# Carrying transposed squares through a DRAM tile with four writes and one read, in place of sixteen SBUF to SBUF transfers

## The chip, the cores and the metric

One core of one Trainium2 chip. The metric is the time of the whole program on the device in microseconds (us), the median of several runs. The program uses one core.

## The reference, cut to what matters

Four graph layers over x of shape (32, 512, 128), all float32. The kernel works on *pairs* of batch items, 16 pairs. Each layer normalizes a pair to h and needs h both with nodes on the partitions (for the products with the adjacency) and with features on the partitions (hT, for the products with weights).

```python
for layer in (L0, L1, L2, L3):
    h = jnp.maximum(_layernorm(x, axis=-1), 0.0)
    x = x + layer(h, adj, ...)
# L0: A*I h W0 + A*(1-I) h W1 ; L1: relu([h, A^T h, (2AA-I)^T h, ...] Theta + b)
# L2: phi2(relu(phi1([ (adj*adj)^T relu(h psi), h ]))) ; L3: tanh/exp attention over h q k^T h^T, masked by adj
```

## The kernel before

`transposed` turns h into hT. VectorE transposes 32x32 squares in place into `hb` (two buffers), and transfers on the SP queue then carry row block i, column block j of the squares to row block j of `hT` (four buffers of 512 KB). That takes sixteen transfers of 32 KB for each of 60 pairs: pairs 4 to 15 of layer 0 (the first four are transposed by TensorE), and all pairs of layers 1 to 3.

```python
def transposed(h, name):
    hb = late.tile([P, NQR, 2, NT, QR], F32, tag="hb", name=f"hb_{name}", bufs=2)
    for b in range(2):
        nc.vector.transpose(hb[:, :, b]..., h[:, b]...)                      # L227
    hT = feature_major(name)                                                 # bufs=4
    for i in range(NQR):
        for j in range(NQR):
            nc.sync.dma_start(hT[j * QR : (j + 1) * QR, i], hb[i * QR : (i + 1) * QR, j])   # L232
    return hT
...
def cross_rows(dst, src):                    # 16 transfers on the same queue, called twice before layer 0
    for a in range(NT):
        for b in range(NQR):
            nc.sync.dma_start(dst[a * QR : (a + 1) * QR, b, :], src[b * QR : (b + 1) * QR, a, :])   # L96
...
def layer0_first(q):
    ln_stats(q);  yield
    h = normed(q);  yield
    hT = (transposed_by_pe if q < EARLY else transposed)(h, f"hT0_{q}");  yield
    g = ...                                  # p_g = hT W1, then evicted to g
    early[q] = hT, g
def layer2(q):
    ...; feat = relu(p_feat + psib)          # p_feat = hT psi: VectorE, then ScalarE
    msgT = mixed(feat, ...)                  # p_msgT on TensorE
    nc.gpsimd.tensor_add(xt[q], xt[q], phi2b[...])
```

In these traces every engine and queue takes its instructions in the order that the compile step gave them; that order follows the program only roughly.

Of the kernel before, what the change touches and what calls it, by code (L numbers as in the profile page):

```python
# [9 lines left out]
F32 = mybir.dt.float32  # L10
# [5 lines left out]
P = 128  # L16
QR = 32
NQR = P // QR
# [6 lines left out]
def kernel(  # L25
# [33 lines left out]
    nc = tc.nc  # L59
# [11 lines left out]
    bounce = ctx.enter_context(tc.tile_pool(name="bounce", bufs=4, space=bass.MemoryType.DRAM))  # L71

    def bank(name):
        return psum.tile([P, 512], F32, tag="bank", name=name)
# [135 lines left out]
    def feature_major(name):  # L210
        return work.tile([P, NQR, 2, P], F32, tag="hT", name=name, bufs=4)
# [10 lines left out]
    def transposed(h, name):  # L222


        hb = late.tile([P, NQR, 2, NT, QR], F32, tag="hb", name=f"hb_{name}", bufs=2)
        for b in range(2):
            nc.vector.transpose(hb[:, :, b].rearrange("p j t r -> p t j r"),  # L227
                                h[:, b].rearrange("p t (j c) -> p t j c", c=QR))
        hT = feature_major(name)
        for i in range(NQR):  # L230
            for j in range(NQR):
                nc.sync.dma_start(hT[j * QR : (j + 1) * QR, i], hb[i * QR : (i + 1) * QR, j])  # L232
        return hT

    def mixed(h, mat, tag, name, copy):
# [26 lines left out]
    def layer0_first(q):  # L262
        ln_stats(q)
        yield
        h = normed(q)
        yield
        hT = (transposed_by_pe if q < EARLY else transposed)(h, f"hT0_{q}")
        yield
        g = work.tile([P, NT, 2, D], F32, tag="g", name=f"g_{q}", bufs=4)
        for b in range(2):  # L270
            pg = projected(f"p_g_{q}_{b}", (at(hT, b), w0[:, 1, :]))
            nc.vector.tensor_copy(g[:, :, b, :], pg)
        early[q] = hT, g
# [144 lines left out]
    p = bank("p_adiag")  # L418
# [15 lines left out]
    p = bank("p_qk_t")  # L434
# [4 lines left out]
    p = bank("p_qk")  # L439
# [36 lines left out]
    def layer1(q):  # L476
        h = normed(q)
        yield
        hT = transposed(h, f"hT1_{q}")
        yield  # L480
        x1T, x2T, hs = [], [], []
        for b in range(2):
            x1T.append(mixed(h[:, b], adj_s, "mT", f"x1T_{q}_{b}", nc.vector.tensor_copy))
            x2T.append(mixed(h[:, b], cheb, "x2T", f"x2T_{q}_{b}", nc.scalar.copy))
            hs.append(straight(hT, b, None, f"hs_{q}_{b}"))
        yield
        for b in range(2):
            po = projected(f"p_l1_{q}_{b}", (columns(hs[b]), th[:, 0, :]), (columns(x1T[b]), th12[:, 0, :]),
                           (columns(x2T[b]), th12[:, 1, :]))
            y = late.tile([P, NT, D], F32, tag="y", name=f"y1_{q}_{b}", bufs=3)  # L490
            nc.vector.tensor_add(y, po, spread(b1, NT))
            nc.vector.scalar_tensor_tensor(xt[q][:, b], y, 0.0, xt[q][:, b], OP.max, OP.add)
        ln_stats(q)

    def layer2(q):
        h = normed(q)
        yield
        hT = transposed(h, f"hT2_{q}")
        yield
        yield  # L500
        feat = []
        for b in range(2):
            pf = projected(f"p_feat_{q}_{b}", (at(hT, b), psi))
            feat.append(late.tile([P, NT, D], F32, tag="y", name=f"feat_{q}_{b}", bufs=3))
            nc.vector.tensor_add(feat[b], pf, spread(psib, NT))
            nc.scalar.activation(feat[b], feat[b], AF.Relu)  # L506
        yield
        msgT = [mixed(feat[b], sq[0], "mT", f"msgT_{q}_{b}", nc.vector.tensor_copy) for b in range(2)]
        nc.gpsimd.tensor_add(xt[q], xt[q], phi2b[:, None, None, :].to_broadcast([P, 2, NT, D]))
        yield  # L510
        h1T = []
        for b in range(2):
            ph = bank(f"p_phi1_{q}_{b}")
            nc.tensor.matmul(ph, phi1[:, 1, :], hT[:, :, b, :], start=True, stop=False)  # L514
            nc.tensor.matmul(ph, phi1[:, 0, :], msgT[b], start=False, stop=True)  # L515
            h1T.append(late.tile([P, N], F32, tag="x2T", name=f"h1T_{q}_{b}"))
            nc.scalar.activation(crossed(h1T[b]), split(ph), AF.Relu, bias=phi1b)
        yield
        for b in range(2):
            po = projected(f"p_l2_{q}_{b}", (columns(h1T[b]), phi2))  # L520
            nc.vector.tensor_add(xt[q][:, b], po, xt[q][:, b])
        ln_stats(q)
# [94 lines left out]
```

## Time and profile before

| | before |
|---|---|
| time, median of 4 runs | 1077.55 us |
| span of the profiled run | 1075.6 us |
| TensorE (PE) busy | 1033.2 us, 96% |
| wait of p_g for hT / of p_msgT for feat | 7.2 us / 7.9 us |
| VectorE's wait for a free hb | 105.0 us |
| SP queue for the squares of a pair | 16 issues, 10.35 us |

TensorE is the bound, so time can change only where TensorE stands still or runs at half rate after standing still. The prediction shows the lines. One more view is used throughout: the length of each stage, read from TensorE's timeline as the distance between the first instruction of one stage and the first of the next (first p_l, first p_x1T, first p_feat, p_feat of the second pair, first p_qkh, end). It includes idle and half-rate time, so a difference of stage lengths is a gain or loss of time, and the differences add up to that of the spans.

### The profile page before, as it was taken

The numbers are of one execution on the slowest core, as the hardware profiler recorded it, in microseconds if no ns is written. First come the engines' busy times: TensorE is split into PE (matmuls) and PEld (weight loads), VectorE is DVE, ScalarE is ACT, GpSimd is POOL, SyncE is SP. The second block draws the span as 40 slices with busy tenths as digits, with TensorE's granted clock in tenths as the row PEclk, the third lists the DMA queues.
The fourth block names the chain that finished last, engine by engine and source line by source line (L and its number), as shares of the span: only waits on it lengthen the run. The fifth ranks groups of instructions, "written<-read, shape, count | busy, mean of one in ns | idle before, by whom it ended". The sixth has DMA issues, their size and how long they took to land.

```text
span 1075.6 us, 14578 instructions
## 1 busy us (share of the span) xinstructions
PE 1033.2 (96%) x4966; PEld 701.7 (65%) x4966; DVE 551.7 (51%) x1280; ACT 413.0 (38%) x877; POOL 233.9 (22%) x214
## 2 busy tenths in 40 slices
PE   4998899999999999999969999999999999999997
PEld 3567799995565655656545555555567777677775
DVE  8924566543243332423433554566676565655443
ACT  5723233501221322213642434322265464655543
POOL 2334244322000000001430111000013232333232
PEclk9898999999999999999989999999999999999999
DMA  9512111110101010010110111111111122122201
GB/s 269 127 47 69 51 51 51 51 52 19 27 25 35 20 34 26 25 34 20 51 29 26 37 39 38 39 40 40 40 31 52 57 61 59 57 62 63 66 30 40
DMA packets 85114, 53.56 MB, mean 50 GB/s; under 512 B 17713, under 2 KB 83505, under 8 KB 85041
## 3 DMA queue, kind: packets, MB, share of 16 engines
q1 hardware_dynamic: 85040, 52.63, 18.1%
q8 instruction: 40, 0.66, 0.3%
q14 instruction: 34, 0.27, 0.1%
HBM read 10.62 MB, written 8.39 MB: 18 GB/s over the span
## 4 chain that ended last, share of the span: by engine, by line
PE 79%; SPq 13%; issue 2%; DMA 2%; ACT 2%; DVE 1%; POOL 0%; POOLq 0%; DVEq 0%; ACTq 0%
PE p_msgT L239 10%; PE p_av L556 10%; PE p_l L255 9%; PE p_x1T L239 9%; PE p_x2T L239 9%; SPq L232 9%; PE p_score L544 8%; PE p_l L468 7%; PE p_phi L514 3%; PE p_feat L255 2%; PE p_phi L515 2%; PE p_qkh L532 2%; PE p_hv L255 2%; SPq L96 2%; PE p_l L470 2%
## 5 line engine op out<-in xcount | busy, mean ns | idle before, releaser
L227 DVE STREAM_TRANSPOSE hb_hT<-h 128x512 f32<-128x512 f32 x120 | 83.7, 703 | 202.3 <-DMA hT<-hb_hT 105.0
L200 ACT ACTIVATE h<-x,sh,rs 128x128 f32<-128x128 f32 x384 | 154.8, 486 | 37.9 <-DVE hb_hT L227 23.3
L549 POOL TENSOR_TENSOR ex<-ex,adjTx 128x512 f32<-128x512 f32 x64 | 85.0, 1330 | 269.5 <-ACT ex L547 257.4
L556 PEld LDWEIGHTS p_av<-hv,ex 128*128 128x128 f32 x1024 | 120.3, 193 | 14.4 <-issue 5.3
L556 PE MATMUL p_av<-hv,ex 128*128 128x129 f32 x1024 | 123.6, 278 | 3.9 <-POOL ex L549 2.7
L468 PE MATMUL p_l<-g,attT 128*128 128x256 f32 x512 | 125.0, 387 | 0.0
L239 PE MATMUL p_msgT<-sq,feat 128*128 128x512 f32 x256 | 115.1, 603 | 7.9 <-ACT feat L506 7.9
L544 PE MATMUL p_score<-qkh,hT 128*128 128x512 f32 x256 | 115.1, 592 | 0.0
L239 PE MATMUL p_x1T<-adj_s,h 128*128 128x512 f32 x256 | 115.1, 592 | 0.0
L239 PE MATMUL p_x2T<-cheb,h 128*128 128x512 f32 x256 | 115.1, 592 | 0.0
L545 ACT ACTIVATE ex<-p_score 128x512 f32<-128x512 f32 x128 | 72.4, 586 | 76.4 <-PE p_score L544 53.1
L468 PEld LDWEIGHTS p_l<-g,attT 128*128 128x128 f32 x512 | 94.3, 195 | 10.5
L239 PEld LDWEIGHTS p_msgT<-sq,feat 128*128 128x128 f32 x256 | 49.5, 194 | 70.4 <-issue 61.6
L183 DVE BATCH_NORM_STATS2 bn<-x 128x6 f32<-128x256 f32 x256 | 92.3, 415 | 1.6
L186 ACT ACTIVATE sd<-bn,eps 128x8 f32<-128x8 f32 x64 | 18.2, 303 | 195.1 <-DVE bn L183 195.0
L239 PEld LDWEIGHTS p_x2T<-cheb,h 128*128 128x128 f32 x256 | 48.6, 190 | 61.2 <-issue 61.0
L239 PEld LDWEIGHTS p_x1T<-adj_s,h 128*128 128x128 f32 x256 | 47.4, 190 | 53.6 <-issue 53.3
L547 ACT ACTIVATE ex<-ex 128x512 f32<-128x512 f32 x128 | 76.5, 629 | 1.6
L544 PEld LDWEIGHTS p_score<-qkh,hT 128*128 128x128 f32 x256 | 46.2, 190 | 46.4 <-issue 42.6
L241 ACT COPY x2T<-p_x2T 128x512 f32<-128x512 f32 x32 | 18.7, 585 | 149.1 <-PE p_x2T L239 149.0
L454 POOL COPY hs<-hT 128x512 f32<-128x512 f32 x32 | 20.1, 629 | 243.5 <-PE p_l L255 243.5
L549 DVE TENSOR_TENSOR ex<-ex,adjTx 128x512 f32<-128x512 f32 x64 | 50.1, 786 | 44.4 <-ACT ex L547 44.4
(129 smaller groups left out, 1392.5 us busy)
## 6 DMA issues: line engine op xcount, KB each, us to landing
hT<-hb_hT SPq DMA_DIRECT2D x960, 32.0 KB, 1.9
x<-in_x_dram SPq DMA_DIRECT2D x32, 256.0 KB, 5.5
out_dram<-x SPq DMA_DIRECT2D x32, 256.0 KB, 2.4
adj_s<-in_adj_dram SPq DMA_DIRECT2D x4, 256.0 KB, 3.3
adjTx<-adjT SPq DMA_DIRECT2D x16, 64.0 KB, 2.0
adjx<-adj_s SPq DMA_DIRECT2D x16, 64.0 KB, 2.0
th<-in_L_gnn_Theta_dram SPq DMA_DIRECT2D x1, 320.0 KB, 6.4
w<-in_L_gnn_W_dram SPq DMA_DIRECT2D x1, 128.0 KB, 4.9
```

Source lines behind the costliest of these rows:

```text
L183: nc.vector.bn_stats(st[:, k].rearrange("p e s -> p (e s)"), xt[q][:, b, t : t + 2, :].rearrange("p t f -> p f t"))
L200: nc.scalar.activation(h[:, b, t, :], xt[q][:, b, t, :], AF.Relu, bias=shift[q][:, i : i + 1], scale=scale[q][:, i : i + 1])
L227: nc.vector.transpose(hb[:, :, b].rearrange("p j t r -> p t j r"), h[:, b].rearrange("p t (j c) -> p t j c", c=QR))
L232: nc.sync.dma_start(hT[j * QR : (j + 1) * QR, i], hb[i * QR : (i + 1) * QR, j])
L239: nc.tensor.matmul(p, h[:, t, :], mat[:, t, :], start=(t == 0), stop=(t == NT - 1))
L255: nc.tensor.matmul(p[:, blk(t)], hT(t), w, start=(i == 0), stop=(i == len(terms) - 1))
L468: nc.tensor.matmul(po[:, i], attT[:, s, blk(t0 + i)], g[:, s], start=(s == 0), stop=False)
L544: nc.tensor.matmul(ps, hT[:, t, b, :], qkh, start=True, stop=True)
L545: nc.scalar.activation(ex[:, t, :], ps, AF.Tanh, scale=1.0 / (8.0 * math.sqrt(D)))
L547: nc.scalar.activation(ex[:, t, :], ex[:, t, :], AF.Exp, scale=8.0)
L549: eng.tensor_mul(ex[:, t, :], ex[:, t, :], adjTx[:, t, :])
L556: nc.tensor.matmul(po[:, i, : D + 1], ex[:, t, blk(i0 + i)], hv[:, t, :], start=(t == 0), stop=(t == NT - 1))
```

## The change

The idea is that the sixteen transfers tie up the queue by their number. The change writes each row block of squares with one transfer of 128 KB into a DRAM tile, already in the wanted order, and fetches the whole of hT with one read of 512 KB. The DRAM tile has four buffers of its own, so a pair can leave `hb` before a buffer of hT is free.

```diff
+        d = bounce.tile([NQR, QR, NQR, 2 * P], F32, tag="d", name=f"d_{name}")
+        for i in range(NQR):
+            nc.sync.dma_start(d[:, :, i, :].rearrange("j c e -> c j e"),
+                              hb[i * QR : (i + 1) * QR].rearrange("c j b t r -> c j (b t r)"))
         hT = feature_major(name)
-        for i in range(NQR):
-            for j in range(NQR):
-                nc.sync.dma_start(hT[j * QR : (j + 1) * QR, i], hb[i * QR : (i + 1) * QR, j])
+        nc.sync.dma_start(hT.rearrange("p i b n -> p (i b n)"), d.rearrange("j c i e -> (j c) (i e)"))
         return hT
```

## The prediction

> **What bounds the kernel now.** I began with the page of the profile, its share of each engine and its slices.
>
> ```profile
> PE 1033.2 (96%) x4966; PEld 701.7 (65%) x4966; DVE 551.7 (51%) x1280; ACT 413.0 (38%) x877; POOL 233.9 (22%) x214
> ...
> PE   4998899999999999999969999999999999999997
> ...
> hT<-hb_hT SPq DMA_DIRECT2D x960, 32.0 KB, 1.9
> ```
>
> TensorE is the bound: 96% of 1075.6 us, and 9 in nearly every slice. So a change to a transfer can only win where PE is not a 9, and lose where it opens new holes. Slices of 26.9 us that are not 9 are the first (start-up), numbers 3 and 4 (81 to 134 us), number 20 (538 to 565 us) and the last (the tail). The table of stages gives PE idle of 16.7 us before 65 us, 8.7 us in 65 to 131, nothing in 131 to 505, 9.0 us in 505 to 560, nothing in 560 to 775, and 8.5 us after 775. The last line above is the changed operation: 960 transfers, sixteen for each of 60 pairs (12 in layer 0, 16 in each later layer).
>
> Second view: what PE waited for. Columns are total us, times, longest.
>
> ```profile
> PE p_msgT L239 <- ACT feat L506: 7.9, 1, 7.9
> PE p_g L255 <- DMA hT<-hb_hT: 7.2, 6, 2.0
> ...
> PE p_adjT L279 <- POOL ident masks.py:199: 5.2, 1, 5.2
> PE p_first L393 <- ACT h L200: 5.0, 1, 5.0
> ```
>
> The second line names the changed transfer outright; it is the hole at 81 to 134 us. The first is the hole at 538 to 565 us and seems to have nothing to do with the change. The other two are start-up and can't move. Third view, the chain of work that ended last, shows what stands behind the first hole:
>
> ```profile
> 549.98 1.67 SPq L232
> ...
> 551.70 1.83 DMA hT<-hb_hT
> ...
> 553.70 1.30 DVE hb_hT L227 x2
> ...
> 558.42 0.61 DVE feat L505
> ...
> 559.05 0.64 ACT feat L506
> ...
> 559.74 9.63 PE p_msgT L239 x16
> ```
>
> Before these lines the chain is an unbroken row of issues of line 232 from 510.6 us on. VectorE waits in order for a free hb buffer (two of them) before it transposes the pair after next; hb comes free only when all sixteen transfers out of it have landed; and the eviction of feat, which PE needs, stands behind that transpose. The same view at the start of layer 0 is again line 232 from 90.3 to 128.3 us.
>
> Fourth view, the timeline of the SP queue and of PE in that stage:
>
> ```profile
> 65.96 10.09 SPq L96 DMA_DIRECT2D adjTx<-adjT  x16
> 76.22 2.40 SPq L232 DMA_DIRECT2D hT<-hb_hT  x4
> 78.81 11.41 SPq L96 DMA_DIRECT2D adjx<-adj_s  x16
> 90.27 54.98 SPq L232 DMA_DIRECT2D hT<-hb_hT  x85
> ```
> ```profile
> 99.33 0.68 PE L255 MATMUL p_g<-w,hT 128*128 128x128 f32 x4 [1.96 <-DMA hT<-hb_hT]
> 101.75 1.19 PE L255 MATMUL p_g<-w,hT 128*128 128x128 f32 x4 [1.74 <-DMA hT<-hb_hT]
> 102.74 3.62 PE L468 MATMUL p_l<-g,attT 128*128 128x256 f32 x8
> ```
>
> The queue issues without a pause: 85 in 54.98 us, 0.647 us each, so 10.35 us for sixteen. A pair costs PE 10.48 us in layer 0 (p_g begins at 152.37, 162.85 and 173.33 us in the chain). The queue is 99% full there and cannot make up the delay that the 32 crossing transfers of the adjacency gave it.
>
> **What the Trainium skill says.** (1) "DMA: Bandwidth & Descriptors", section "Issuing engines are not separate DMA queues", calls the sequencer time of starting a transfer "usually small relative to the DMA itself". This trace disagrees for these small transfers: 0.647 us per issue makes 10.35 us for a pair against 1.9 us to landing, so issuing is the cost. (2) The same page, "Anatomy of one DMA", gives a fixed 2.0 us plus bytes at 436 GB/s, fixed part mostly the receipt. Near it: 1.9 us for 32 KB here, and 2.4 us for the 256 KB outputs (the formula says 2.6). (3) The same page, "Two DMAs through the same engine are not ordered", says a transfer that reads what another wrote must be held at the issuing engine until the first has signalled completion. So the read costs the SP queue a full landing of the writes; no run before has such a pair. (4) "TensorE: Matmul & The Clock Gate", Part 1, says an idle window drops the array to half rate until it has been busy for some 3.4 us. The trace agrees: the eight matmuls at 102.74 take 3.41 us start to end less the modelled overlap, the same eight at 154.16 take 1.73.
>
> **The change, part by part.**
>
> Issues removed: sixteen a pair, 16 x 0.647 = 10.35 us of queue. The 1.9 us landing of the last follows, so hT is whole some 12.2 us after hb.
>
> Issues added: five. Their cost I take from transfers with one end in DRAM: the outputs of line 563 (also 512 rows each) take a median 378 ns against 589 ns for line 232; loads at the very start take about 0.43. With 0.04 us between, some 0.45 each. Four writes of 128 KB: 3 x 0.45 = 1.35 us to the last issue, then its landing. I take 2.3 us (between 1.9 for 32 KB and 2.4 for 256 KB), then 0.45 for the read: the queue is held 1.35 + 2.3 + 0.45 = 4.1 us a pair, 6.2 less. The landing of a 512 KB read: 1.9 fixed plus 512 KB at the 269 GB/s of the first slice (1.95) is 3.8 us at worst; the skill's formula gives 3.2. I take 3.5. Whole latency: 4.1 + 3.5 - 0.45 = about 7.2 us against 12.2. hb is free at 3.7 us instead of 12.2.
>
> Traffic: 60 x 0.52 MB = 31.5 MB written and as much read in DRAM; that queue's 52.63 MB and 18.1% become 84 MB and, in proportion, 29%. Not a bound.
>
> Moved: with sixteen transfers the first quarter of p_g could begin after four landed; with one read nothing can begin before all is there. This costs nothing where hT is early, which is everywhere but in the two holes.
>
> Gain in 68.1 to 131.6 us: PE ran 160 records of L468 (0.2166 us at full rate), 80 of L470 (0.111) and 64 of L255 (0.112): 34.7 + 8.9 + 7.2 = 50.8 us in 63.5. Of the 12.7 lost, 0.7 waits for POOL; 12.0 is line 232, of it 7.2 idle and 4.8 slow clock. In the new order I expect the four writes in the place of the four transfers at 76.2 us (between the two crossings, where the queue has to wait for the first to land), then sixteen adjx, then the read at 90.3, landed by 94.3. PE comes to this p_g at 95.6 us. Each later pair takes the queue 4.1 us of a 10.48 us period, so it arrives early. All of the 12.0 us goes, with a margin of only 1.3 us on the first pair.
>
> Gain around 550 us: idle 1.1 (a late x2T eviction on ACT, itself behind VectorE's wait) plus 7.9, plus slow clock, p_msgT 9.5 us for 16 instead of 6.87: 2.6. Sum 11.6. Without the wait on hb, y, x, feat and relu of the last layer-1 pair (0.6 + 0.7 + 0.6 + 0.6 us) still lie between p_l and p_msgT, with PE having 1.8 us of p_feat to cover them: about 1 us stays. Gain 10.6.
>
> Layers 1, 2 and 3 in their steady part: PE has no hole, a pair takes 19.1, 13.9 and 17.5 us against 4.1 of queue. VectorE's 105 us of waiting for hb shrinks, and is worth nothing there. Sum: 12.0 + 10.6 = 22.6 us, so 1055.5 us if all of it comes.
>
> **The rivals.** (A) Only part comes: the compile order of the queue and of VectorE changes, the read is put behind something slow (in layer 3 an output that waits for VectorE, 10.7 us at longest; in layer 0 the crossing transfers), or PE meets p_g sooner. For it: a single read has to wait for all four writes and blocks the queue; the margin of 1.3 us is thin. Against: 6.2 us a pair of room. Result 1060 to 1070. (B) The round trip takes the place of the issues: if writes to DRAM land in 4 to 5 us and the read in 5 or more (as loads at the start did, 5.5 us at 269 GB/s, though in a full queue), latency is 11 us or over and the holes stay: 1072 to 1082. Against: 256 KB outputs land in 2.4. (C) Another wait appears where hT buffers (four) are given back late, because one read needs the whole buffer: the SP queue already waits 74 us for p_phi there, and PE showed no hole; a few us, 1062 to 1075.
>
> **Range and chances.** The full sum gives 1055.5; the 2% line is 1078.06 x 0.98 = 1056.5, so faster needs 21.6 of 22.6 us. I give the full sum (within a us) one chance in three, a loss of some us to A or C over half, B one in ten. I predict 1058 us, range 1052 to 1071; faster 0.34, same 0.62, slower 0.04.
>
> **What would show it.** Right: 60 reads and 240 writes; issue of some 0.45 us; write landings near 2.3, read near 3.5; the SP queue waiting for its own writes about 2 us sixty times; the wait of p_g for hT and of p_msgT for feat gone or under 1 us each; VectorE's wait for hb far below 105 us; slices 3, 4 and 20 of PE at 9; PE busy some 7 us less, as slow matmuls go. Wrong: write or read landings over 5 us, issues over 1 us, or a new PE wait in layers 2 or 3 behind a read that stands after an output.

## The result, and the profile after

The median is 1063.59 us (4 runs, 1062.4 to 1065.08) against 1077.55: ratio 0.9865, 95% interval 0.984 to 0.989. Ratios here and below are the mean time of one kernel's runs over that of the other's of the same rounds, so not quite the ratio of the medians quoted. The gain is clear, and under 2%.

The page of the kernel after, engines, slices and the two transfers (out<-in, count, KB each, us to landing):

```profile
PE 1025.7 (97%) x4966; PEld 698.4 (66%) x4966; DVE 561.5 (53%) x1280; ACT 413.7 (39%) x877; POOL 233.4 (22%) x214
...
PE   4996999999999999999989999999999999999997
...
d_hT<-hb_hT SPq DMA_DIRECT2D x240, 128.0 KB, 2.4
hT<-d_hT SPq DMA_DIRECT2D x60, 512.0 KB, 3.3
```

PE does the same 4966 instructions in 7.5 us less (fewer at half rate). Slice 20 (counted from 0) rose from 6 to 8 and slice 4 from 8 to 9, but slice 3 fell from 8 to 6: one hole became deeper and shorter. What PE waited for (total us, times, longest), after:

```profile
PE p_g L257 <- DMA hT<-d_hT: 8.4, 1, 8.4
...
PE p_msgT L241 <- ACT feat L508: 3.2, 1, 3.2
```

The wait for hT has not gone: six short waits of 7.2 us became a single one of 8.4. The timelines of the SP queue and of PE around it (start, us, what, count; in brackets idle time and what ended it):

```profile
65.32 10.09 SPq L96 DMA_DIRECT2D adjTx<-adjT  x16
75.58 0.95 SPq L231 DMA_DIRECT2D d_hT<-hb_hT  x2
76.94 10.34 SPq L96 DMA_DIRECT2D adjx<-adj_s  x16
87.33 2.07 SPq L231 DMA_DIRECT2D d_hT<-hb_hT  x4
90.38 0.34 SPq L234 DMA_DIRECT2D hT<-d_hT  x1
```
```profile
85.39 0.61 PE L472 MATMUL p_l<-w,hd 128*128 128x128 f32 x4
94.40 3.78 PE L257 MATMUL p_g<-w,hT 128*128 128x128 f32 x16 [8.40 <-DMA hT<-d_hT]
```

The read goes out at 90.38 and PE has the data at 94.40, almost to the tenth what was predicted (90.3, 94.3). That is luck: the crossing transfers ended 3 us earlier than was assumed (87.28 us), but only two of the pair's four writes had gone out ahead of them, and the other two and their landing cost 3 us again. And PE comes to p_g at 86.0 us, not at 95.6. Its sixteen records then take 3.78 us in place of 1.95 (half rate).

The SP queue's own waits, and VectorE's for a buffer to transpose into (the latter was 105.0 us):

```profile
SPq L234 <- DMA d_hT<-hb_hT: 54.0, 49, 3.6
```
```profile
DVE hb_hT L227 <- DMA d_hT<-hb_hT: 2.1, 2, 1.9
```

So the round trip costs the queue 54 us of waiting over 60 pairs, and VectorE hardly waits for hb at all.

Stage lengths of the profiled runs, with the changed terms of the prediction beside them:

| stage | before | after | gain | predicted gain |
|---|---|---|---|---|
| start-up | 68.10 | 67.46 | 0.64 | 0 |
| layer 0 | 174.86 | 172.75 | 2.11 | 12.0 |
| layer 1, and start of layer 2 | 306.96 + 19.29 | 305.49 + 13.50 | 7.26 | 10.6 |
| rest of layer 2 | 206.31 | 206.31 | 0.00 | 0 |
| layer 3 and tail | 300.07 | 295.70 | 4.37 | 0 |
| sum | 1075.60 | 1061.22 | 14.38 | 22.6 |

The start-up lies between 67.5 and 70.0 us in all the profiles below, so 0.64 there is nothing.

### The profile page after: what moved, and what is told of

It is laid out like the page before. It is cut to its first block, busy times and chain, and to the rows that moved or that the text cites. A ratio compares the mean times of both kernels' runs of the same rounds, so it can differ in the third digit from the quotient of the medians.

```text
span 1061.2 us, 13502 instructions
## 1 busy us (share of the span) xinstructions
PE 1025.7 (97%) x4966; PEld 698.4 (66%) x4966; DVE 561.5 (53%) x1280; ACT 413.7 (39%) x877; POOL 233.4 (22%) x214
## 4 chain that ended last, share of the span: by engine, by line
PE 89%; SPq 4%; DMA 2%; ACT 2%; issue 2%; DVE 1%; POOL 0%; POOLq 0%; DVEq 0%; ACTq 0%
PE p_msgT L241 11%; PE p_x1T L241 10%; PE p_x2T L241 10%; PE p_l L257 10%; PE p_av L558 10%; PE p_score L546 10%; PE p_l L470 9%; PE p_feat L257 3%; PE p_hv L257 3%; PE p_phi L516 3%; PE p_phi L517 3%; PE p_qkh L534 2%; PE p_g L257 2%; PE p_l L472 2%; SPq L96 2%; SPq L108 2%
## 5 line engine op out<-in xcount | busy, mean ns | idle before, releaser
L558 PE MATMUL p_av<-hv,ex 128*128 128x129 f32 x1024 | 121.3, 275 | 2.3 <-POOL ex L551 2.0
L470 PE MATMUL p_l<-g,attT 128*128 128x256 f32 x512 | 122.0, 381 | 0.0
L551 DVE TENSOR_TENSOR ex<-ex,adjTx 128x512 f32<-128x512 f32 x64 | 45.8, 716 | 65.5 <-ACT ex L549 65.5
L243 DVE COPY x1T<-p_x1T 128x512 f32<-128x512 f32 x32 | 22.1, 691 | 99.8 <-PE p_x1T L241 99.8
```

The source lines that it names most:

```text
L243: copy(s, p)
L470: nc.tensor.matmul(po[:, i], attT[:, s, blk(t0 + i)], g[:, s], start=(s == 0), stop=False)
L551: eng.tensor_mul(ex[:, t, :], ex[:, t, :], adjTx[:, t, :])
L558: nc.tensor.matmul(po[:, i, : D + 1], ex[:, t, blk(i0 + i)], hv[:, t, :], start=(t == 0), stop=(t == NT - 1))
```

## The experiments

Times are medians of 4 runs each; ratios are to the kernel before, timed in the same rounds on one chip (1077.99 us in the first set, 1077.64 in the second, which shares runs with it). All results were correct. The stage lengths are told at the end.

### TensorE meets p_g of pair 4 one step later (a_pg_later)

```diff
@@ layer0_first, changed kernel
         yield
+        if q == EARLY:
+            yield
         g = work.tile([P, NT, 2, D], F32, tag="g", name=f"g_{q}", bufs=4)
```

> The changed kernel, with the p_g matmuls of pair 4 alone put one step later in the program, so that TensorE does the eight matmul groups of layer-0 pair 2 first. The crossing transfers and the DRAM path stay as they are. Theory (what failed in the prediction is only where TensorE meets p_g of pair 4: at 85.8 us, where I had put it at 95.6, while the read lands at 94.2 as predicted): TensorE comes about 8.7 us later, the wait of 8.4 us of p_g for hT falls under 1 us and the half-rate matmuls behind it (about 2.8 us) go too: 10 to 11 us under the changed kernel, about 1053 us. Rival (the round trip through DRAM is itself too slow for layer 0, so later pairs will wait in its place): a wait of several us appears at p_g of pair 5 or 6, gain under 4 us, 1060 us or more.

Measured 1063.39 us where about 1053 was expected, ratio 0.9863: no gain over the change. The aimed-at wait did what the theory said, yet another took its place. PE, then SP:

```profile
97.91 2.05 PE L257 MATMUL p_g<-w,hT 128*128 128x128 f32 x16 [0.67 <-DMA hT<-d_hT]
106.40 3.75 PE L257 MATMUL p_g<-w,hT 128*128 128x128 f32 x16 [6.44 <-DMA hT<-d_hT]
```
```profile
94.10 7.83 SPq L231 DMA_DIRECT2D d_hT<-hb_hT  x4
102.11 0.34 SPq L234 DMA_DIRECT2D hT<-d_hT  x1
```

Pair 4 now waits 0.67 us, pair 5 then 6.44. The four writes in the first row of the last fence are two of pair 5 and two of pair 6: in the order of the compiled queue, two writes of pair 6 stand ahead of the read of pair 5. They wait for pair 6's transposes, which VectorE starts at 99.8 us, and the read waits behind them. Here the rival's sign came (a wait at pair 5), but for another reason than a slow round trip: one queue in order, with the next pair's writes ahead of this pair's read.

### The crossing transfers moved out of the way (a_cross_late, b_cross_late)

```diff
@@ both kernels
-    adjTx = square_tile("adjTx")
-    cross_rows(adjTx, adjT)
-    adjx = square_tile("adjx")
-    cross_rows(adjx, adj_s)
+    late_adj = {}
+    def crossings():
+        late_adj["T"] = square_tile("adjTx")
+        cross_rows(late_adj["T"], adjT)
+        yield
+        late_adj["x"] = square_tile("adjx")
+        cross_rows(late_adj["x"], adj_s)
@@ uses of adjTx, adjx become late_adj["T"], late_adj["x"]
+    waiting[NQ + 2].append(crossings())
```

> The changed kernel, with the 32 crossing transfers of the adjacency moved from before layer 0 into a generator that starts with layer 1 (the compile order then strews them between the transfers of layer 0 where the queue has room). Theory (the read of pair 4 is late because it stands behind sixteen crossing transfers of 0.65 us each on the queue): the read goes out before 80 us, lands before TensorE comes to it at 86, the wait of 8.4 us and its half-rate tail vanish, 1051 to 1054 us. Rival (the write-wait-read chain is what makes it late): the wait stays at 4 us or more, 1058 to 1064 us.

Measured 1055.44 us, ratio 0.9796 (0.9775 to 0.9816), somewhat over the expected 1051 to 1054. The SP queue:

```profile
70.03 1.78 SPq L231 DMA_DIRECT2D d_hT<-hb_hT  x4
71.86 1.79 SPq L96 DMA_DIRECT2D adjTx<-adjT  x3
73.95 0.35 SPq L234 DMA_DIRECT2D hT<-d_hT  x1
```

The read of pair 4 goes out at 73.95 us, and PE does that p_g without waiting. Layer 0 takes 163.77 us instead of 172.75. The wait of 8.4 us was the place in the queue, not the length of the round trip. A wait of 2.0 us, which was not foreseen, remains at p_g of pair 5: in the compiled order a write of pair 6 again stands ahead of the read of pair 5.

> The kernel before with the 32 crossing transfers moved into the generator at the start of layer 1, as in a_cross_late (the compile order strews them over layer 0 between the sixteen direct transfers of each pair). Theory (the queue is full in layer 0 with direct transfers: 12 pairs x 10.35 us plus 32 x 0.65 = 145 us from 66 us on against 126 us of TensorE's work, so the crossings only move the shortage to later pairs): layer 0 still loses 6 us or more in waits of p_g or hd for hT, and the holes of layers 2 and 3 stay: 1070 to 1077 us. Rival (the crossings in front alone make the hole, the path of the squares does not matter there): layer 0 shortens by about 10 us, 1066 us.

Measured 1078.94 us (1070 to 1077 expected), ratio 1.002 (0.9992 to 1.0047). With direct transfers the same move gains nothing:

```profile
PE p_g L255 <- DMA hT<-hb_hT: 9.2, 5, 3.3
```

The five waits now lie between 98 and 173 us, so the shortage is only handed on to later pairs, as the sum of issues said. Moving the crossings pays only on a queue that has room, and the change is what makes the room.

### Direct transfers on two queues (b_actq), and the DRAM path with sixteen writes (a_16w)

```diff
@@ b_actq: the kernel before
-                nc.sync.dma_start(hT[j * QR : (j + 1) * QR, i], hb[i * QR : (i + 1) * QR, j])
+                eng = nc.scalar if j % 2 else nc.sync
+                eng.dma_start(hT[j * QR : (j + 1) * QR, i], hb[i * QR : (i + 1) * QR, j])
@@ a_16w: the changed kernel
-            nc.sync.dma_start(d[:, :, i, :].rearrange("j c e -> c j e"),
-                              hb[i * QR : (i + 1) * QR].rearrange("c j b t r -> c j (b t r)"))
+            for j in range(NQR):
+                nc.sync.dma_start(d[j, :, i, :], hb[i * QR : (i + 1) * QR, j].rearrange("c b t r -> c (b t r)"))
```

> The kernel before, sixteen direct transfers a pair, but every second one issued from ScalarE's queue. Theory (what costs is the issue time on one queue, not the path): the SP queue holds a pair for some 5.2 us instead of 10.35, the hole around 550 us shrinks from 11.6 to 2 to 6 us and the hole of layer 0 by several us, unless the 480 issues at 0.6 us that ScalarE now does (some 290 us on an engine busy 413 of 1076) delay its own evictions: 1060 to 1072 us. Rival (the gain needs the DRAM tile, which lets go of hb before hT has a free buffer): 1074 us or more.

> The changed kernel with each of the four writes of a pair cut into four (sixteen writes of 32 KB and one read, the same bytes over the same DRAM tile). Theory (number of issues on the queue): 16 x 0.44 + 2 + 0.4 = about 9.4 us of queue a pair and some 13 us to hT, as in the kernel before; most of the gain is lost, 1070 to 1080 us, with a wait of p_g for hT of 8 us or more in layer 0 and of p_msgT of 5 us or more. Rival (the path over DRAM, by letting go of hb early, is what gains): 1062 to 1066 us.

b_actq: 1066.58 us, ratio 0.9895. a_16w: 1070.99 us, ratio 0.9936. Read by stage, the two separate what the totals mix:

- In layer 0 the number of issues on the queue matters: with the same path, sixteen writes in place of four lengthen it from 172.75 to 182.68 us (a_16w, with one wait of p_g of 13.1 us). It is not the count alone, for a_16w is also slower than the kernel before (174.86), where p_g could begin on its first quarter. b_actq, with half of the transfers on SP, takes 166.02 us.
- At the start of layer 2 either is enough: b_actq takes 13.79 us and a_16w 10.16, against 19.29 before. The theory had expected p_msgT in a_16w to wait 5 us or more; it waits 1.2. This half of the theory fell: sixteen writes over DRAM already free hb early enough there.
- In layer 3 the number of writes to DRAM does not matter: a_16w takes 295.71 us, as the changed kernel. b_actq takes 299.08, close to 300.07, but that says little of the path: of its 49.6 us of waiting for hb only 3.7 fall in layer 3 (50.2 in the kernel before), and where PE waits at the start of the layer (2.3 us) it waits for ex, which ScalarE makes between its own issues. What the path does in layer 3 is tested below (d_not3).

Why the path matters there is argued in part. The record shows that with the DRAM tile the transposes run ahead: the last one starts at 798.9 us, in the kernel before at 983.6 us, so that later in layer 3 VectorE has none left to wait for. One would think that a direct transfer must wait for a free hT buffer before it can empty hb. At the first place where PE lost time in layer 3 of the kernel before (790 us) the chain runs from PE over ScalarE's ex back to transfers that had indeed waited 3.7 us for such a buffer; VectorE itself waited only 1.3 us for hb there. At the two others (913 and 932 us) the queue had waited at most 0.4 us for a buffer: there the sixteen transfers stood behind an output that waited 6.8 us for VectorE, and VectorE then waited 5.0 and 4.6 us for hb. The queue of the kernel before:

```profile
891.00 7.82 SPq L563 DMA_DIRECT2D out_dram<-x  x2
898.91 10.87 SPq L232 DMA_DIRECT2D hT<-hb_hT  x16
```

No run takes one of these causes away alone, and none gives hb more buffers in SBUF, which might let the transposes run ahead without DRAM. b_actq also pays for its second queue: ScalarE is now held up by its own issues, and PE waits 2.9 us for x2T in layer 1, whose stage grows from 306.96 to 308.88 us.

### Layer 3 with direct transfers (d_not3)

```diff
@@ transposed, changed kernel: after the two transposes
+        if name.startswith("hT3"):
+            hT = feature_major(name)
+            ...the sixteen direct transfers...
+            return hT
```

> The changed kernel, but layer 3 keeps the sixteen direct transfers. Theory (the unforeseen 4.4 us gained in layer 3 come from VectorE no longer waiting in order for a free hb, at 785 to 797 and at 930 us of the kernel before): layer 3 takes 299 to 300 us again instead of 295.7, VectorE waits for hb for 40 us or more, the time is 4 to 5 us over the changed kernel, 1067 to 1069 us. Rival (layer 3 is shorter only because it starts in another order or phase): layer 3 stays at 296 us, 1063 to 1065 us.

Measured 1072.46 us (1067 to 1069 expected), ratio 0.9944. Layer 3 grows from 295.70 to 303.94 us, 8.2 us where 4 to 5 were expected (even 3.9 us over the kernel before), and the other stages stay as after the change. VectorE and PE:

```profile
DVE hb_hT L227 <- DMA hT<-hb_hT: 54.5, 13, 6.6
```
```profile
PE p_av L564 <- DVE qkh L542: 3.9, 3, 1.5
```

VectorE stands before a transpose waiting for hb, behind it stand the evictions of qkh and the products of ex, and PE then waits for those. The gain of layer 3 is thus due to the path in layer 3 itself.

### The read from another queue (a_late_rpool)

```diff
@@ a_cross_late
-        nc.sync.dma_start(hT.rearrange("p i b n -> p (i b n)"), ...)
+        nc.gpsimd.dma_start(hT.rearrange("p i b n -> p (i b n)"), ...)
```

> a_cross_late with the one read of each pair issued from GpSimd's queue instead of SP's, so that no read can stand behind the next pair's writes and SP never waits for a landing. Theory (the 2.0 us that p_g of pair 5 still waits in a_cross_late, and the 6.4 us in a_pg_later, come from a write of the next pair that stands ahead of the read in the one queue and waits for its transpose): the wait of p_g for hT is gone, layer 0 about 3 us shorter, 1051 to 1053 us, unless GpSimd, which now waits in order for the writes, is late with hd, hs or ex. Rival (GpSimd's waits cost more than they save): new waits of TensorE for hd or ex, 1056 us or more.

Measured 1055.13 us (1051 to 1053 expected), ratio 0.979, the same as a_cross_late (0.9796). SP no longer waits for landings, but the wait at p_g of pair 5 rose from 2.0 to 3.9 us and layer 0 from 163.77 to 167.19. GpSimd has an order of its own:

```profile
93.45 2.36 POOL L468 TENSOR_TENSOR x<-x,b 128x1024 f32<-128x1024 f32 x1 [4.01 <-ACT h L200]
95.75 0.60 POOL L234 DMA_DIRECT2D hT<-d_hT  x1
```

The read of pair 5 stood behind an addition that waited for ScalarE. The theory's cure failed: the read was put behind other work, not freed. (The start of layer 2 became 3.3 us shorter in exchange. Its trace shows why: GpSimd came later to its addition there, 0.37 us after VectorE's x update had begun, and that update took 0.69 us in place of 2.48; the next section tells of this.)

### GpSimd's addition in halves (a_late_ph)

What is left of the hole at the start of layer 2 shows in the timelines of VectorE and GpSimd after the change:

```profile
543.22 0.69 DVE L493 TENSOR_TENSOR y<-p_l,b 128x512 f32<-128x512 f32 x1 [4.21 <-PE p_l L257]
543.95 2.48 DVE L494 SCALAR_TENSOR_TENSOR x<-y,x 128x512 f32<-128x512 f32 x1
...
549.42 0.68 DVE L507 TENSOR_TENSOR feat<-p_feat,psib 128x512 f32<-128x512 f32 x1
```
```profile
543.51 2.37 POOL L511 TENSOR_TENSOR x<-x,phi2b 128x1024 f32<-128x1024 f32 x1 [4.88 <-ACT h L200]
```

The x update takes 0.69 us in most places; here it takes 2.48 and ends 0.55 us after GpSimd's addition, which began first. The Trainium skill, page "SBUF — State Buffer", section "Who interferes with whom", says that VectorE and GpSimd share one pair of SBUF ports under an exclusive lock, and that a VectorE instruction with both inputs in SBUF is blocked whole while a GpSimd instruction that reads SBUF holds it. Both inputs of the update (y and x) are in SBUF.

```diff
@@ layer2, on a_cross_late
-        nc.gpsimd.tensor_add(xt[q], xt[q], phi2b[:, None, None, :].to_broadcast([P, 2, NT, D]))
+        for b in range(2):
+            nc.gpsimd.tensor_add(xt[q][:, b], xt[q][:, b], spread(phi2b, NT))
```

> a_cross_late with GpSimd's addition of phi2b to x (128x1024, 2.35 us) cut in two halves. Theory (of the 3.2 us that p_msgT still waits at the start of layer 2, about 2.2 is VectorE's x update, which takes 2.48 us in place of 0.69 while GpSimd's addition holds the SBUF port that both need): the longest x update falls to 1.4 us or less, the wait to 1 to 2.3 us, the time 1 to 3 us under a_cross_late. Rival (the long x update has another cause, or the halves follow each other and hold the port as long): x update still over 2 us, wait 3 us, same time.

Measured 1054.05 us, ratio 0.9779 (0.9763 to 0.9796). The update of that place, and the wait:

```profile
535.95 1.39 DVE L498 SCALAR_TENSOR_TENSOR x<-y,x 128x512 f32<-128x512 f32 x1
```
```profile
PE p_msgT L241 <- ACT feat L512: 2.1, 1, 2.1
```

The update fell from 2.48 to 1.39 us, the wait from 3.2 to 2.1, the stage from 13.69 to 12.70. The update again ends 0.55 us after the GpSimd instruction beside it, and in a_late_rpool and a_16w, where GpSimd's addition began after the update, it took 0.69. All of this supports the lock. (The longest x update of the run, at another place, took 1.49 us, a little over the expected 1.4.) The interval overlaps that of a_cross_late, so the gain of 1 us is shown by the stage, not by the totals. This kernel has the lowest median: 2.2% under the kernel before, and about 0.9% under the change by their ratios (0.9779 against 0.9865).

### All by stage

Stage lengths in us, profiled runs. "Layer 1 +" ends at the first p_feat, "start 2" at the p_feat of the second pair; the rest of layer 2 is 206.31 in every run.

| kernel | layer 0 | layer 1 + | start 2 | layer 3 | median time |
|---|---|---|---|---|---|
| before | 174.86 | 306.96 | 19.29 | 300.07 | 1077.55 |
| after | 172.75 | 305.49 | 13.50 | 295.70 | 1063.59 |
| a_pg_later | 171.11 | 305.49 | 15.05 | 295.55 | 1063.39 |
| a_cross_late | 163.77 | 305.49 | 13.69 | 295.54 | 1055.44 |
| b_cross_late | 175.35 | 307.17 | 19.62 | 299.55 | 1078.94 |
| b_actq | 166.02 | 308.88 | 13.79 | 299.08 | 1066.58 |
| a_16w | 182.68 | 305.49 | 10.16 | 295.71 | 1070.99 |
| d_not3 | 173.07 | 305.49 | 13.72 | 303.94 | 1072.46 |
| a_late_rpool | 167.19 | 305.49 | 10.37 | 295.88 | 1055.13 |
| a_late_ph | 163.78 | 305.49 | 12.70 | 295.54 | 1054.05 |

## Why the prediction was right, and where it was not

The time (1063.59) lies in the range and the call "within 2%" held, but the sum got there partly because errors of opposite sign met: layer 0 gave 9.9 us less than predicted and the start of layer 2 gave 3.3 less, layer 3 gave 4.4 more. What came is rival A, a loss of part of the gain, which the prediction had given over half of its chances.

- **Costs of the transfers: right.** Writes landed in 2.4 us (2.3 predicted), the read in 3.3 (3.5), read and writes were issued in 0.34 and a median 0.43 us. Rival B (a slow round trip) is out. The SP queue's wait for its own writes was predicted as "about 2 us sixty times" and was 54 us in 49 waits, since other work often stood between. The formula that the prediction takes from the skill is stated there for transfers that GpSimd issues; that it came near for transfers of the SP queue is a finding of this trace. Its reading that the trace agrees with the skill on the clock holds for the factor of two; here the half rate came after waits of 1.96 and 1.74 us with four matmuls between, and no wholly idle 3.4 us was needed.
- **Layer 0: the step that failed** is "PE comes to this p_g at 95.6 us". PE came at 86.0, found nothing, and waited 8.4 us; of 12.0 us only 2.1 came. At 95.6 the kernel before did the second quarter of this p_g; its first quarter stood at 86.48 us, for it could begin after four of sixteen transfers. One read makes all of p_g wait for everything, and the compile order put all of p_g where the first quarter had been. The prediction named the lost quarter and said that it "costs nothing where hT is early, which is everywhere but in the two holes" — this was one of the holes. Rival A named it too ("or PE meets p_g sooner"). a_cross_late showed that the data need not be late: with the read in front of the crossings layer 0 gave 11.1 us (174.86 to 163.77).
- **Start of layer 2: mechanism right, size off.** Of 10.6 us 7.3 came. The remaining wait was put at about 1 us and was 3.2; VectorE's x update, assumed at 0.7 us, took 2.48 beside GpSimd. a_16w, whose update is not hit, waits 1.2 us, as the prediction had it.
- **Layer 3: a term of 0 that measured 4.4.** The prediction said of VectorE's wait for hb that it "is worth nothing there". It stood in the way of qkh at two places of the kernel before, where PE waited 0.35 (at 913 us) and 0.53 us (932), and, less clearly, of ex at 790 us, where PE waited 1.5 us and half-rate matmuls followed (granted clock 0.93 in 775 to 800 us, 1.00 in 900 to 1000). The prediction had 8.5 us of PE idle after 775 us in its table and put all of it down to the tail; 3.7 us of it were waits between matmuls. d_not3 showed the cause: give layer 3 the direct transfers back, and the loss returns.
- **What carried the gain.** b_actq shows that nearly as much (ratio 0.9895 against 0.9865) can be had without DRAM, by a shorter queue, though not at the same places: it gains 8.8 us in layer 0, where the change gained 2.1, and 1.0 in layer 3, where the change gained 4.4. On the one queue the gain of layer 3 needs the DRAM path: sixteen writes to DRAM keep it (a_16w), sixteen direct transfers lose it (d_not3).

What stays open: why layer 3 with direct transfers behind DRAM layers (d_not3) is 3.9 us slower than in the kernel before, and what ties hb in layer 3: the free hT buffer, the outputs that stand in the same queue, or both.

## What to carry to other kernels

Count the issues on a queue against the period of the bounding engine: here sixteen issues made 10.35 us of a 10.48 us period, and a queue so full did not make up its delay (b_cross_late); fewer and larger transfers gave it room even at the price of a round trip through DRAM. When many small transfers become one, ask where the first consumer meets the *first* part, for that is where the whole must now be. And a wait of an engine that is not the bound is worth nothing only if nothing that the bound needs stands behind it in the same queue.

## What the Trainium skill lacked or had wrong

- "DMA: Bandwidth & Descriptors", section "Issuing engines are not separate DMA queues", says that a second issuing engine saves only sequencer time, "usually small relative to the DMA itself". For 32 KB transfers it was not small: 0.647 us of queue each, a third of the 1.9 us to landing, and 10.35 us for sixteen, which follow one another; a second queue alone gained 1% (ratio 0.9895).
- The same page has no issue times by kind of transfer for this chip. Medians here on the SP queue: SBUF to SBUF of 32 KB 589 ns, SBUF to DRAM of 128 KB 433 ns, of 256 KB 378 ns, DRAM to SBUF of 512 KB 338 ns. At the same 32 KB and from the same tile, a write to DRAM (a_16w) took 419 ns against 589 to SBUF, so the destination matters; among the writes the size mattered little. That is not the whole story: the loads of x at the start, 256 KB each from DRAM, took a median 821 ns.
- The formula of the same page (2.0 us plus bytes at 436 GB/s), which it states for transfers issued from GpSimd, came near for the larger transfers issued from SP: 2.4 us for the 128 KB writes (2.3 by the formula), 3.3 for the 512 KB reads (3.2). It is too high for small ones: the 32 KB writes of a_16w landed in 1.6 us (2.1). The 512 KB reads that GpSimd issued (a_late_rpool) took 3.6.
- No page gives the cost, to the transfers behind it, of one that waits in an issuing queue: 6.4 us of TensorE idle in a_pg_later, from writes of the next pair that waited for their transposes ahead of a read.
- The lock of "SBUF — State Buffer" agreed: 2.48 us for a VectorE update of 0.69 us, beside 2.37 us on GpSimd.
